# Additions of whole graphs by accumulating DMAs, and one more halving of row sums, in a four-layer graph network on one core

## The chip, the cores and the metric

The kernel runs on one core of a Trainium2 chip. Times are device microseconds (us). A core has five engines that run side by side, each working through its own instructions in a fixed order: TensorE (PE, matrix products; PEld is its weight load), VectorE (DVE), ScalarE (ACT), GpSimd (POOL) and SyncE (SP, which only issues DMAs here). An engine waits for others by semaphores. DMAs are issued by SP and POOL and are carried out by 16 DMA engines. [...]

## The reference

32 graphs of 512 nodes with 256 features pass through four layers. They share one adjacency matrix of 512 by 512. Each layer's output is added to its input and normalised over the features.

```python
# layer 0: attention with 8 heads, then a two-layer perceptron, each with residual and layernorm
scores = jnp.where(mask, jnp.einsum('fnhd,fmhd->fhnm', q, k) / jnp.sqrt(D), -1e9)
t = jnp.einsum('fhnm,fmhd->fnhd', jax.nn.softmax(scores, axis=-1), v).reshape(F, N, C)
x = _layernorm(x + t, ln1_g, ln1_b)
h = jax.nn.relu(jnp.einsum('fnc,cd->fnd', x, w1) + b1)
x = _layernorm(x + jnp.einsum('fnd,dc->fnc', h, w2) + b2, ln2_g, ln2_b)
...
# layer 1: e = leaky_relu(s1[n] + s2[m]), masked softmax, times h, one head
# layer 2: e = leaky_relu(h1 h2^T), masked softmax, times h3, relu
# layer 3: as layer 1 with 4 heads of 64 features, then elu
...
# around every layer
x = _layernorm(x + layer(x))
```

## The kernel before

One graph is held as tiles of 128 partitions: a tile [128, 4, 256] has node 128c + p of the graph in partition p and part c. One such tile (kinds "x" and "y") is 512 KB. Attention weights of four blocks are held as a tile [128, 4, 512] of kind "p", 1 MB. Everything is float32, and every product is made of two records of PE. A PSUM bank ("bank") takes one result of [128, 512].

`graph(b)` loads one graph by SP, runs `layer0` to `layer3`, each followed by `normalise`, and stores the result by SP. `normalise` takes statistics on DVE (L906, L907), a power of -1/2 on POOL (L909, L910), a product on DVE (L911), and applies them on ACT (L914).

What belongs to the change:

- `add` (L918) is an addition or product on POOL of two of the four parts of a tile, so a whole tile takes two. It is used in layer 0 for the residual (`t + xs`), for `xs + be2_row`, for `n1 * g1_row` and for `y + bb_row`; in layers 2 and 3 for the residual (`y + xs`). The result is read by DVE: by the statistics L906, by L1085 (`f = product + y`), by L1095 (`f + xs`), and by L1279 (the last step of the elu in layer 3).
- `add_dma` (L927) adds one "p" tile to another by an accumulating DMA of 1 MB issued by POOL. Layer 0 uses it to sum the exponentials over the blocks of source nodes (six times a graph), layer 3 twice a graph.
- The row sums of the softmax are column sums of those totals over the partitions, made on PE: L1041 in layer 0 and L1266 in layer 3. In layer 3 a total holds two blocks of two heads each, and eight products with 32 columns of weights (`pick`) leave the two blocks of a head in separate rows. After a transposition `rinv3` adds the two on DVE (L960) and takes the reciprocal (L964).
- The product of weights and values is L1024 in layer 0 (32 columns of weights each) and L1251 in layer 3 (64 columns each). The attention scores of layer 0 are L995 (32 rows). All other products use the whole array.

The order of work is not that of the program text. Every step is handed to `plan` with its engine, a price in ns, what it reads and writes, for some a `lag` (how long after the issue the result is believed to be there) and for PE a number `tiling` for the mode of the array. `Plan.place` then simulates the engines and writes down their order: it takes the engine that can start first, and on it the step with the earliest start and, among equals, the earliest due time. A step whose `tiling` differs from the mode that PE is in has `STAY` added to its due time, and is believed to cost 100 ns more. Up to `WAYS` = 5 graphs are in flight; graph b + 5 begins when graph b has ended. Due times come from `PACE`, `TENTHS` and `LAST`, first starts from `START`. On the chip the engines keep this order and wait for the true ends of what they need.

Before the graphs, `prepare` loads weights and the adjacency (`load`, L727) and derives tables from them, among them edge_t from transpositions at L766 and a product of two weights of layer 2 from transpositions at L830.

Of the kernel before, what the change touches and what calls it, by code (L numbers as in the profile page):

```python
# [13 lines left out]
ALU = mybir.AluOpType  # L14
# [3 lines left out]
P = 128  # L18
# [8 lines left out]
WAYS = 5  # L27
PACE = 94.27
START = (0, 0, 51.94, 76.72, 152.79)
LAST = ()  # L30
STAY = 4.37
TENTHS = (0, 52.5, 93.97, 124.51, 191.84, 234.11, 292.66, 343.39, 414.47, 446.08, 504.73)
@with_exitstack
# [578 lines left out]
def fast_path(  # L612
# [86 lines left out]
    def T(slot):  # L699
        return slot.tile if slot.kind is None else buffers[slot.kind][slot.index]  # L700
# [25 lines left out]
    def prepare():  # L726
        def load(dst, to, src, lag=3000):  # L727
            def run():
                with nc.allow_non_contiguous_dma(reason="columns, once"):
                    nc.sync.dma_start(to(T(dst[0] if isinstance(dst, tuple) else dst)), src)  # L730
            plan(SP, 60, run, [], [dst], lag=lag)

# [193 lines left out]

    def add_dma(dst, src):  # L927

        plan(POOL, 950, lambda: nc.gpsimd.dma_start(T(dst), T(src), accum_op=ALU.add),  # L929
             [src, dst], [dst], lag=7000)  # L930

# [21 lines left out]
    def rinv3(sm):  # L953


        bank, rinv = sums_back(sm), Slot("ri")

        def run():
            r = T(rinv)[:, :NC * H3]
            nc.vector.tensor_reduce(  # L960
                r.rearrange("p (c k i) -> p c k i", c=NC, k=KC),
                T(bank).rearrange("p (c a i r) -> p c r i a", c=NC, a=2, i=2)[:, :, 0:KC],
                mybir.AxisListType.X, ALU.add)
            nc.vector.reciprocal(r, r)  # L964
        dve(400, run, [bank], [rinv])
        return rinv
# [36 lines left out]
    def layer0(xs):  # L1003
# [47 lines left out]
        dve(370, check, [rinv], [], True)  # L1051
        for c0 in range(0, NC, 2):
            add(t, t, xs, c0)
        n1 = Slot("y")
        normalise(t, n1)
        for c0 in range(0, NC, 2):
            add(xs, xs, None, c0, be2_row)
        nT = transposed(n1)
        y = Slot("y")
        for c0 in range(0, NC, 2):  # L1060
            add(y, n1, None, c0, g1_row, ALU.mult)
            add(y, y, None, c0, bb_row)
        hT = Slot("t")
# [36 lines left out]
    def gates(v, heads, G):  # L1100
# [5 lines left out]
        def check():  # L1106
# [11 lines left out]
            [bank], [gT])  # L1118
        plan(SP, 60, lambda: nc.sync.dma_start(T(row)[:R, :], T(gT)[:R, :]), [gT], [row], lag=2000)
        if heads == 1:  # L1120
            to = lambda: T(G)
        else:
            to = lambda: flat(T(G))
        plan(SP, 60, lambda: nc.sync.dma_start(
            to(), T(row)[:R, :].rearrange("r q -> (r q)").partition_broadcast(P)),
            [row], [G], lag=2300 + 1100 * heads)
        e1, e02 = Slot("e1"), Slot("e1")
# [35 lines left out]
    def layer2(xs):  # L1163
# [40 lines left out]
        for c0 in range(0, NC, 2):  # L1204
# [10 lines left out]
            for j in range(2):  # L1215
                act(470, lambda bank=bank, j=j, c=c0 + j: nc.scalar.activation(
                    T(y)[:, c, :], T(bank)[:, j * C:(j + 1) * C], AF.Relu,
                    scale=T(rinvs[c])[:, 0:1]), [bank, rinvs[c0 + j]], [(y, c0 + j)])
            add(y, y, xs, c0)
        return y  # L1220

    def layer3(xs):
# [5 lines left out]
        for k in range(KC):  # L1228
            av = Slot("bank")
            for m0 in range(0, NC, 2):  # L1230
# [16 lines left out]
                def run(p=p, m0=m0, k=k, av=av):  # L1247
                    for m in range(2):
                        for i in range(2):
# [4 lines left out]
                                             stop=(m0 + m == NC - 1))  # L1254
                plan(PE, 1770, run, [q, p], [av], tiling=2)
                if m0 == 0:
                    total = p
                else:
                    add_dma(total, p)

            totals.append(total)
            evac(oT, lambda t, k=k: t[:, k, :], av, lambda b: b, N, [(oT, k)])
        def run():
            for k, p in enumerate(totals):
                for j in range(4):
                    nc.tensor.matmul(T(sm)[32 * j:32 * j + 32, :], pick[:, k, :], T(p)[:, j, :],  # L1266
                                     start=(k == 0), stop=(k == KC - 1))
        plan(PE, 1740, run, totals, [sm], tiling=2)
        t = heads_out(oT, rinv3(sm), H3)

        e, y = Slot("y"), Slot("y")
        for c0 in range(0, NC, 2):
            w, parts = slice(c0, c0 + 2), (c0, c0 + 1)
            act(600, lambda w=w: nc.scalar.activation(T(e)[:, w, :], T(t)[:, w, :], AF.Exp),
                [(t, c) for c in parts], [(e, c) for c in parts])
            act(600, lambda w=w: nc.scalar.activation(T(y)[:, w, :], T(t)[:, w, :], AF.Relu),
                [(t, c) for c in parts], [(y, c) for c in parts])
            add(y, y, xs, c0)
            dve(790, lambda w=w: nc.vector.scalar_tensor_tensor(  # L1279
                T(y)[:, w, :], T(e)[:, w, :], 1.0, T(y)[:, w, :], ALU.min, ALU.add),  # L1280
                [(s, c) for s in (y, e) for c in parts], [(y, c) for c in parts], True)
        return y

    def graph(b):
        xs = Slot("x")
        plan(SP, 60, lambda xs=xs: nc.sync.dma_start(
            T(xs), x[b].rearrange("(c p) d -> p c d", p=P)), [], [(xs, c) for c in range(NC)],
            lag=11000)
        for layer in (layer0, layer1, layer2, layer3):
            y = layer(xs)  # L1290
            xs = Slot("x")
            normalise(y, xs)
        plan(SP, 60, lambda: nc.sync.dma_start(
            out[b].rearrange("(c p) d -> p c d", p=P), T(xs)), [xs], [], lag=3000)
# [79 lines left out]
```

## Time and profile before

| | |
|---|---|
| median of 3 runs | 3067.17 us (3066.87 to 3067.29) |
| profiled execution | 3065.91 us |
| its span, first to last instruction | 3064.1 us |
| mean granted TensorE clock | 0.989 |
| PE idle in the span | 120 us |
| DVE busy | 2313.2 us (75%) |
| POOL busy | 1368.9 us (45%) |

The page has one line per engine with its busy time, its share of the span and its number of instructions, then the span in 40 slices with the busy share of each in tenths, then groups of instructions: source line, engine, operation, output and input, shapes and count, busy us, mean ns of one, and after the second bar the idle time just before them with what ended most of it. DMA issues show the size of one and the median time from issue to landing.

Three facts help in reading it. A group's line can be that of a helper: all of POOL's additions have L921. A POOL record of a DMA is the time of its issue, not of the transfer. And idle time of an engine that sets no end costs nothing.

### The profile page before, as it was taken

How to read it: one execution, taken by the hardware profiler on the slowest of the kernel's cores; microseconds unless marked ns; L12 is line 12 of the kernel's file. 1: busy time of each engine (PE TensorE's matmuls, PEld its weight loads, DVE VectorE, ACT ScalarE, POOL GpSimd, SP SyncE). 2: the span in 40 equal slices, each digit the busy share in tenths (PEclk: the TensorE clock that was granted, in tenths of full speed). 3: DMA queues.
4: the chain of work that ended last, by engine and by line, in shares of the span. 5: the costliest groups of instructions: out<-in, count | busy, mean ns of one | idle time of the engine just before them, and what ended most of it. 6: DMA issues, size and time to landing. Idle time of an engine off the chain costs nothing.

```text
span 3064.1 us, 41217 instructions
## 1 busy us (share of the span) xinstructions
PE 2943.6 (96%) x14954; PEld 1650.4 (54%) x14954; DVE 2313.2 (75%) x4170; ACT 1890.3 (62%) x3975; POOL 1368.9 (45%) x1195
## 2 busy tenths in 40 slices
PE   6989999999999999999999999999999999999994
PEld 3455555555555555555555555555555555555551
DVE  4667777777777777777777777778777778777774
ACT  4656666666666666666666666566766666666552
POOL 0433455444455444455444455444455444454422
PEclk9999999999999999999999999999999999999997
DMA  5644654555654555654555654555655555655323
GB/s 149 131 85 100 141 117 94 126 116 114 141 118 93 126 116 114 141 117 96 127 113 114 141 116 95 116 122 118 135 110 107 114 122 119 132 113 107 80 75 82
DMA packets 85939, 351.65 MB, mean 115 GB/s; under 512 B 7905, under 2 KB 43873, under 8 KB 48865
## 3 DMA queue, kind: packets, MB, share of 16 engines
q0 software_dynamic: 36864, 268.45, 44.6%
q1 hardware_dynamic: 48864, 80.49, 7.5%
q8 instruction: 120, 1.97, 0.3%
q14 instruction: 91, 0.74, 0.1%
HBM read 63.38 MB, written 17.10 MB: 26 GB/s over the span
## 4 chain that ended last, share of the span: by engine, by line
PE 73%; DMA 17%; DVE 5%; ACT 3%; issue 2%; POOL 0%; SPq 0%; POOLq 0%; DVEq 0%; ACTq 0%
DMA p<-p 15%; PE bank L878 9%; PE bank L892 8%; PE bank L995 8%; PE bank L1152 8%; PE bank L1211 7%; PE bank L1024 6%; PE bank L1251 6%; PE bank L1069 4%; PE bank L865 4%; PE bank L1081 4%; DVE p L1017 2%; PE bank L1266 2%; ACT p L999 2%; PE bank L978 2%; PE bank L1200 2%
## 5 line engine op out<-in xcount | busy, mean ns | idle before, releaser
L1017 DVE TENSOR_TENSOR p<-p,edge_t 128x2048 f32<-128x2048 f32 x256 | 625.5, 2446 | 225.1 <-ACT p L999 221.4
L929 POOL DMA_DIRECT2D p<-p x256 | 239.2, 935 | 895.5 <-PE bank L1251 159.8
L853 ACT ACTIVATE t<-bank 128x512 f32<-128x512 f32 x640 | 371.0, 595 | 415.7 <-PE bank L878 162.3
L999 ACT ACTIVATE p<-bank 128x512 f32<-128x512 f32 x1024 | 533.0, 603 | 99.0 <-PE bank L995 98.7
L921 POOL TENSOR_TENSOR y<-y,x 128x512 f32<-128x512 f32 x192 | 321.9, 1735 | 313.6 <-DVE y L981 239.1
L906 DVE BATCH_NORM_STATS2 st<-y 128x6 f32<-128x256 f32 x768 | 314.7, 410 | 11.4 <-POOL y L921 3.6
L995 PE MATMUL bank<-t,t 32*128 32x512 f32 x2048 | 301.8, 644 | 0.0
L1242 DVE TENSOR_TENSOR p<-p,edge_t 128x2048 f32<-128x2048 f32 x128 | 294.1, 2298 | 4.2
L914 ACT ACTIVATE x<-y,rs,rs 128x256 f32<-128x256 f32 x512 | 276.0, 591 | 25.2 <-DVE rs L911 24.2
L1235 DVE TENSOR_SCALAR p<-p,e,e 128x512 f32<-128x512 f32 x512 | 256.9, 541 | 39.6 <-DMA p<-row 39.6
L1024 PE MATMUL bank<-p,v 128*32 128x512 f32 x2048 | 269.7, 608 | 10.5 <-DVE p L1017 10.3
L1251 PE MATMUL bank<-p,v 128*64 128x512 f32 x1024 | 252.6, 615 | 22.7 <-DVE p L1242 22.6
L909 POOL TENSOR_SCALAR rs<-mv 128x4 f32<-128x4 f32 x192 | 161.5, 841 | 223.9 <-DVE mv L907 211.5
L1152 PE MATMUL bank<-v,p 128*128 128x257 f32 x1024 | 249.4, 389 | 6.9 <-DVE p L1145 6.9
L1152 PEld LDWEIGHTS bank<-v,p 128*128 128x128 f32 x1024 | 189.1, 191 | 88.7 <-issue 24.4
L1211 PE MATMUL bank<-v,p 128*128 128x256 f32 x1024 | 235.2, 383 | 0.0
L878 PE MATMUL bank<-t,wqkv 128*128 128x512 f32 x512 | 227.1, 594 | 0.0
L1177 PE MATMUL bank<-t,t 128*128 128x512 f32 x512 | 225.1, 592 | 0.0
L1211 PEld LDWEIGHTS bank<-v,p 128*128 128x128 f32 x1024 | 192.6, 191 | 47.8 <-ACT t L853 20.5
L853 ACT ACTIVATE v<-bank 128x512 f32<-128x512 f32 (+2 forms) x384 | 176.5, 461 | 64.5 <-PE bank L892 32.0
L910 POOL TENSOR_TENSOR rs<-rs,mhalf 128x4 f32<-128x4 f32 x192 | 207.6, 1081 | 16.0
L921 POOL TENSOR_TENSOR y<-y,bb_row 128x512 f32<-128x512 f32 x64 | 186.4, 2912 | 4.9
(117 smaller groups left out, 4636.7 us busy)
## 6 DMA issues: line engine op xcount, KB each, us to landing
p<-p POOLq DMA_DIRECT2D x256, 1024.0 KB, 8.0
p<-row SPq DMA_DIRECT2D x32, 1024.0 KB, 9.4
x<-in_x_dram SPq DMA_DIRECT2D x32, 512.0 KB, 8.3
out_dram<-x SPq DMA_DIRECT2D x32, 512.0 KB, 2.9
e<-row SPq DMA_DIRECT2D x32, 256.0 KB, 3.5
t<-in_adj_dram SPq DMA_DIRECT2D x4, 256.0 KB, 6.0
wqkv<-in_L_gnn_w_qkv_dram SPq DMA_DIRECT2D x1, 768.0 KB
y<-in_L_gnn_W_dram SPq DMA_DIRECT2D x2, 256.0 KB
```

Source lines behind the costliest of these rows:

```text
L853: act(170 + n * 0.84, lambda: nc.scalar.activation(to(T(dst)), frm(T(src)), AF.Copy), [src], writes)
L878: nc.tensor.matmul(T(bank), T(w)[:, i, col:col + P], T(xT)[:, i, :], start=(i == 0), stop=(i == KC - 1))
L906: nc.vector.bn_stats(T(st)[:, c, :], T(y)[:, c, :])
L921: pool(1500 if row is None else 1850, lambda: nc.gpsimd.tensor_tensor(T(dst)[:, w, :], T(a)[:, w, :], T(b)[:, w, :] if row is None else T( ...
L995: nc.tensor.matmul(T(banks[j]), T(kT)[r, g, m * P:(m + 1) * P], T(qT)[r, g, :], start=True, stop=True)
L999: act(600, lambda j=j: nc.scalar.activation(T(p)[:, j, :], T(banks[j]), AF.Exp, scale=1.0 / math.sqrt(D0)), [banks[j]], [(p, j)])
L1017: dve(2420, lambda p=p, m=m: nc.vector.tensor_tensor(T(p), T(p), T(edge_t)[:, m, :].unsqueeze(1).to_broadcast([P, J, N]), ALU.mult), [p, ( ...
L1024: nc.tensor.matmul(T(av)[j * D0:(j + 1) * D0, :], T(v)[:, m, h * D0:(h + 1) * D0], T(p)[:, j, :], start=(m == 0), stop=(m == NC - 1))
L1152: nc.tensor.matmul(T(bank)[:, :C + 1], T(p)[:, m, c * P:(c + 1) * P], T(v)[:, m, 2:C + 3], start=(m == 0), stop=(m == NC - 1))
L1211: nc.tensor.matmul(T(bank)[:, j * C:(j + 1) * C], T(pT)[:, m, c * P:(c + 1) * P], T(v)[:, m, :C], start=(m == 0), stop=(m == NC - 1))
L1242: nc.vector.tensor_tensor(p4, p4, T(edge_t)[:, m0:m0 + 2, :].unsqueeze(2).to_broadcast([P, 2, 2, N]), ALU.mult)
L1251: nc.tensor.matmul(T(av)[i * D3:(i + 1) * D3, :], T(q)[:, m0 + m, 2 * H3 + h * D3:2 * H3 + (h + 1) * D3], T(p)[:, 2 * m + i, :], start=(m0 ...
```

## The change

- `add_dma` can now take a whole tile of kind "x" or "y", a row that is repeated for all four parts (`row=True`), or no source: then it adds blocks 2 and 3 of a tile to its blocks 0 and 1.
- Five additions of each graph that POOL made in two halves each become one accumulating DMA of 512 KB: `t + xs`, `xs + be2_row` and `y + bb_row` in layer 0, `y + xs` in layers 2 and 3. The product with `g1_row` stays on POOL.
- In layer 3 each of the two totals is halved once more by an accumulating DMA of 512 KB, issued behind the first. The row sums then take four products instead of eight, and `rinv3` takes the reciprocal alone.
- L1251 has a mode number of its own for the planner (`tiling=3`).
- The planner's prices change: an SP issue from 60 to 450 ns; the default lag of weight loads from 3 to 15 us; a graph's load from 11 to 9 us; accumulating DMAs from 7 to 7.5 us (1 MB) and 5.5 (512 KB); the broadcast of a row of gates from 2300 + 1100 per head to 1500 + 1900 per head. `PACE`, `START`, `LAST`, `STAY` and `TENTHS` have new values.

```diff
-PACE = 94.27
-START = (0, 0, 51.94, 76.72, 152.79)
-LAST = ()
-STAY = 4.37
+PACE = 97.38
+START = (0, 0, 23.42, 89.7, 132.67)
+LAST = (0.95, 0, 4.11, 0)
+STAY = 7.12
...
-        def load(dst, to, src, lag=3000):
+        def load(dst, to, src, lag=15000):
...
-            plan(SP, 60, run, [], [dst], lag=lag)
+            plan(SP, 450, run, [], [dst], lag=lag)
...
-    def add_dma(dst, src):
-
-        plan(POOL, 950, lambda: nc.gpsimd.dma_start(T(dst), T(src), accum_op=ALU.add),
-             [src, dst], [dst], lag=7000)
+    def add_dma(dst, src, row=False, lag=7500):
+
+        def run():
+            a = T(dst) if src else T(dst)[:, 0:2, :]
+            b = T(src) if src else T(dst)[:, 2:4, :]
+            nc.gpsimd.dma_start(a, b.unsqueeze(1).to_broadcast([P, NC, C]) if row else b,
+                                accum_op=ALU.add)
+        plan(POOL, 950, run, [src, dst] if src else [dst], [dst], lag=lag)
...
-        def run():
-            r = T(rinv)[:, :NC * H3]
-            nc.vector.tensor_reduce(
-                r.rearrange("p (c k i) -> p c k i", c=NC, k=KC),
-                T(bank).rearrange("p (c a i r) -> p c r i a", c=NC, a=2, i=2)[:, :, 0:KC],
-                mybir.AxisListType.X, ALU.add)
-            nc.vector.reciprocal(r, r)
-        dve(400, run, [bank], [rinv])
+        dve(250, lambda: nc.vector.reciprocal(
+            T(rinv)[:, :NC * H3], T(bank).rearrange("p (s r) -> p s r", r=32)[:, :, 0]),
+            [bank], [rinv])
...
-        for c0 in range(0, NC, 2):
-            add(t, t, xs, c0)
+        add_dma(t, xs, lag=5500)
...
-        for c0 in range(0, NC, 2):
-            add(xs, xs, None, c0, be2_row)
+        add_dma(xs, be2_row, True, 5500)
...
             add(y, n1, None, c0, g1_row, ALU.mult)
-            add(y, y, None, c0, bb_row)
+        add_dma(y, bb_row, True, 5500)
...
-            add(y, y, xs, c0)
+        add_dma(y, xs, lag=5500)
...
-                plan(PE, 1770, run, [q, p], [av], tiling=2)
+                plan(PE, 1770, run, [q, p], [av], tiling=3)
                 if m0 == 0:
                     total = p
                 else:
                     add_dma(total, p)
+                    add_dma(total, None, lag=5500)
...
-            for k, p in enumerate(totals):
-                for j in range(4):
-                    nc.tensor.matmul(T(sm)[32 * j:32 * j + 32, :], pick[:, k, :], T(p)[:, j, :],
-                                     start=(k == 0), stop=(k == KC - 1))
-        plan(PE, 1740, run, totals, [sm], tiling=2)
+            for h in range(H3):
+                nc.tensor.matmul(T(sm)[32 * h:32 * h + 32, :], pick[:, 0, :],
+                                 T(totals[h // 2])[:, h % 2, :], start=True, stop=True)
+        plan(PE, 870, run, totals, [sm], tiling=2)
...
-            add(y, y, xs, c0)
-            dve(790, lambda w=w: nc.vector.scalar_tensor_tensor(
+        add_dma(y, xs, lag=5500)
+        for c0 in range(0, NC, 2):
+            w, parts = slice(c0, c0 + 2), (c0, c0 + 1)
+            dve(690, lambda w=w: nc.vector.scalar_tensor_tensor(
                 T(y)[:, w, :], T(e)[:, w, :], 1.0, T(y)[:, w, :], ALU.min, ALU.add),
                 [(s, c) for s in (y, e) for c in parts], [(y, c) for c in parts], True)
```

## The prediction

> **What bounds the kernel now.** I read the page's first two parts (busy times, and the span in 40 slices), then the table of stages, then the groups of instructions, the waits and the end of the chain.
>
> ```profile
> span 3064.1 us, 41217 instructions
> PE 2943.6 (96%) x14954; PEld 1650.4 (54%) x14954; DVE 2313.2 (75%) x4170; ACT 1890.3 (62%) x3975; POOL 1368.9 (45%) x1195
> ...
> PE   6989999999999999999999999999999999999994
> ```
>
> ```profile
> 0.00:20.00 20.00, 1.40 (x7) 1.43 (x8) 2.82 (x9) 1.94 (x3) 1.09 (x11) 1.00 0.88 262
> 500.00:700.00 200.00, 198.50 (x1035) 111.61 (x1035) 155.54 (x279) 129.51 (x271) 97.59 (x82) 1.00 0.54 116
> 3020.00:3040.00 20.00, 12.96 (x42) 2.94 (x42) 15.11 (x18) 1.19 (x2) 1.84 (x2) 0.70 0.50 112
> ```
>
> The columns of a stage are its length, then busy us of PE, PEld, DVE, ACT and POOL, the granted clock, the DMA share and GB/s. TensorE (PE) is the bound: it idles 120 us of 3064 (3064.1 - 2943.6). Adding the stages, about 39 us of that lie before 200 us, 46 after 2900, and only 35 in the 2600 us between, where a graph leaves every 92.2 us (outputs start at 447.80 and 2844.87, 26 graphs apart). So in the middle only three things move the time: PE work, PE's own overhead, and new waits of PE. GpSimd (POOL), at 45%, is no bound.
>
> ```profile
> L921 POOL TENSOR_TENSOR y<-y,x 128x512 f32<-128x512 f32 x192 | 321.9, 1735 | 313.6 <-DVE y L981 239.1
> L921 POOL TENSOR_TENSOR y<-y,bb_row 128x512 f32<-128x512 f32 x64 | 186.4, 2912 | 4.9
> L929 POOL DMA_DIRECT2D p<-p x256 | 239.2, 935 | 895.5 <-PE bank L1251 159.8
> ...
> p<-p POOLq DMA_DIRECT2D x256, 1024.0 KB, 8.0
> ```
>
> ```profile
> PE bank L1041 <- DMA p<-p: 22.0, 24, 3.5
> ```
>
> ```profile
> q0 software_dynamic: 36864, 268.45, 44.6%
> ```
>
> These are groups and DMA issues of the page, one line of the waits (us, times, longest) and one of the queues. To be seen: what POOL's additions cost, what an accumulating DMA costs POOL (0.935 us) and until it lands (8.0 us), and that the one steady wait of PE that is of any size, 22.0 of 35 us, is already a wait for accumulating DMAs, at the row sums of layer 0.
>
> **What the Trainium skill says.** "TensorEngine Tiling (Array Packing)", Key Properties: changing the tiling mode drains TensorE. The trace agrees: eight records of L1024 take 0.99 us to the next start when another mode follows (1500.92 to 1501.91), sixteen in one mode take 1.86 (1528.71 to 1530.57), so eight without a change cost 0.87 and a change about 0.12 us. "DMA: Bandwidth & Descriptors", Anatomy of one DMA, gives 2.0 us plus bytes over 436e3 for a DMA from GpSimd: 4.4 us for 1 MB. The trace has 8.0, so I use the trace's. The same section says that DMA engines do not wait on semaphores, the issuing sequencer does; the trace agrees: POOL stood 157.7 us in 35 waits of an accumulating DMA for the one before. "GPSIMD Engine Reference", Specifications, says GpSimd's SBUF interface is shared with VectorE; L1279, which runs beside POOL's additions, took from 657 to 1755 ns, which fits.
>
> **The change part by part.**
>
> *Row sums of layer 3 (L1266).* 16 records a graph become 8. At 1514.27 sixteen take 1.83 us to the next start; eight, with the same change of mode behind them, cost the 0.99 of above. Saved 0.84 us on the bound engine, times 32: **-27 us**. No cover can hide a saving on PE in the middle. The DVE reduction L960 (0.19 us each) goes too, on an engine at 75%: nothing.
>
> *The second halving and five whole-graph additions.* Per graph POOL loses ten additions, in the groups 321.9 + 186.4 + 128.8 = 637 us in all, and issues seven more DMAs, 224 x 0.935 = 209 us: POOL falls to about 941 us (31%). The two DMAs that repeat a row have 1 KB pieces instead of 4 KB; their issue is not in the trace. Bounds: 0.85 us (the shortest issue seen) to 3.7 (four times 0.935, if it goes by pieces); I take 0.935. At the upper end POOL gets 64 x 2.8 = 180 us back, still under 37%. Nothing on PE either way.
>
> *Their landing.* q0's share makes 0.446 x 3064.1 / 256 = 5.34 us of all 16 engines for 1 MB, so an 8.0 us landing (shortest 6.9) is 5.34 plus 1.6 to 2.7. For 0.5 MB: 2.67 plus the same, 4.3 to 5.3; the page's fit would give 3.2 as a lower end, the 1 MB row 8.0 as the upper. I take 5.3. The load of q0 goes from 8 x 5.34 = 42.7 us a graph to 42.7 + 7 x 2.67 = 61.4, 64% of the time, or 67% if small pieces cost half as much again; with SP's queue the engines go from 0.54 to about 0.74.
>
> *The chain of one graph.* A residual that POOL added pair by pair behind its producer (1.7 us, the next instruction already beginning on the first pair) now waits for all four parts and 5.3 us. Three of these lie on the graph's chain (after layer 0's attention, after layers 2 and 3), about +4.5 us each; the bias rows lie beside transposes and two products (L1069 and L1081, over 7 us of PE) and are covered. The halving adds 5.3. So a graph's chain grows by some 19 us. Five graphs are in flight, and one stays 452 us (363.26 to 815.43), while graph 0 went through in 356 us with less company (1.75 to 357.38): in the middle there is slack, so nothing is charged there. At the end there is none:
>
> ```profile
> 3035.69 7.06 DMA p<-p
> 3042.80 1.98 PE bank L1266 x8
> ...
> 3049.41 1.27 POOL y L921
> 3050.71 2.34 DVE y L1279 x2
> ```
>
> The halving puts 5.3 us behind 3042.75 and takes 1.0 from L1266: +4.3. The last residual goes from 3049.41 + 1.27 to a DMA issued at about 3050.4 and landed at 3055.7, then two L1279 at 0.69: 3057.1 where it was 3053.05, +4. Layer 2's residual of the last graph, on the chain at 2994.35, adds 4.5; the L1266 at 3001.62 gives 1.7 back, and some rearranging I put at 1: **+10 us**.
>
> *The order.* It is written by the planner from its prices, so every changed price reorders all engines. Two effects can be priced. First, weights: loads at default lag are now believed to land at 15 us plus 0.45 per issue, not 3 plus 0.06. PE's first instruction now waits for such a load until 18.60 (L830), while x of graph 0 (issued 1.75, 8.3 us to landing) and the adjacency (last L758 at 9.49, 0.43 long) were there at about 10. With the new prices those come first: up to -8.5 us of starting delay, if the ramp hands it on. Bounds 0 and -8.5; I take **-7**. Second, L1251 (64 columns) now counts as its own mode. In the listing of PE from 1499.53 to 1592.1 I count 30 changes of mode, 3 of them between L1251 and the 32-column ones, which the old planner took for none. Half of them saved: 1.5 x 0.12 x 32 = 6; it could also cost as much. I take **-3**. The prices of SP's issues add no instruction: nothing on the chip.
>
> *New waits in the middle.* DVE now waits for DMAs at L906, L1085, L1095 and L1279 where it waited for POOL; queued behind a waiting DVE are L1017 and L1242, which PE needs. PE waits at L1266 for a longer row of DMAs. On POOL, the powers L910 stand behind any issue that waits for a DMA. The new lags (7.5 us for 1 MB, 5.5 for 0.5, each behind 0.95 of issue: 8.45 and 6.45) lie above 8.0 and 5.3, so the order leaves room for some lateness. Bounds: -10 (the present 22.0 us at L1041 half gone) to +70 (below). I take **+2**.
>
> Sum: -27 + 10 - 7 - 3 + 2 = **-25 us**. The profiled execution took 3065.91 (its span 3064.1 and 1.8 around it): 3041. The median shown is 1.3 above that one: 3042.
>
> **The rivals.** *The DMAs become PE's wait* (the slower side). q0 serves one accumulating DMA behind another; in this profile a sum at 1545.42 took 11.32 us and the one chained to it 8.23. At 64% instead of 45% such lateness is more usual, and PE keeps its order. Price: L1041's wait doubles (0.7 us a graph, 22.0 / 32), L1266 gets one of 1.0, and three late residuals on DVE pass 0.3 on: 2.0 x 32 = 64 us. With -27 - 7 - 3 + 10 this makes +37: 3104. It decides from 0.84 us a graph (27 us), where it eats the sums. For it: 1545.42. Against it: L1266 waited for a DMA only at the very end, 3.0 us.
>
> *The gain is only handed back*: added waits of about 0.8 us a graph, or a ramp that keeps none of the 7 us and an end longer by 15. Within 6 us of 3067.
>
> *The new order is much better*: of 30 changes of mode a graph five go (0.6 us x 32 = 19), and the last graphs spread their load: 3042 - 24 = 3018. For it: a change costs 0.12 us, 30 of them 3.6 of 92.2. Against: most follow from the work itself.
>
> That the change doesn't do what it says is out for the sums: L1266's loop is over four heads instead of eight tiles.
>
> **How the numbers follow.** Forecast (3042, own range 3026 to 3058) 0.48; better order (3018) 0.13; handed back 0.11; DMAs as the wait (3104, spread 3075 to 3120) 0.28. This measurement can tell about 0.2%, 6 us. Faster: 0.61; same 0.11; slower 0.28. For 8 in 10 I cut half of the better order's lower tail and about half of the slow case: 3012 to 3100.
>
> **What would show it.** Right: L1266 at x256 with about half of 63.5 us; PE busy near 2943.6 - 30; PE's first record near 10 us; q0 near 64%; POOL near 31%; a graph every 91.2 us or less in the middle; the tail from the last sums to the end longer by 8. Wrong: PE's idle time between 300 and 2900 well over 35 us with p<-p or y as releaser, or DVE idle for DMA at L906 and L1279 and PE behind it at L1024 or L1251.

## The result, and the profile after

| | before | after |
|---|---|---|
| median | 3067.02 us (3066.82 to 3067.29, 4 runs) | 3244.72 us (3243.13 to 3244.84, 4 runs) |
| profiled execution / span | 3065.91 / 3064.1 us | 3244.68 / 3242.9 us |
| mean granted clock | 0.989 | 0.962 |
| PE busy, idle in the span | 2943.6, 120.5 us | 2986.1, 256.8 us |

The ratio is 1.0578 [1.056, 1.0596]: the kernel became 5.8% slower, where 0.8% faster was forecast. The lines moved a little: L1266 (row sums of layer 3) is now L1261, L1251 is L1246, L1017 is L1014, L929 (the accumulating DMAs) is L932, L1279 is L1276; L906 to L921 stayed.

First the page of after: its span and busy times, q0's line, one group, and four of the DMA issues (number, size, median us from issue to landing).

```profile
span 3242.9 us, 41072 instructions
PE 2986.1 (92%) x14698; PEld 1670.9 (52%) x14698; DVE 2232.2 (69%) x4138; ACT 1865.5 (58%) x3975; POOL 960.8 (30%) x1099
...
q0 software_dynamic: 93696, 385.91, 62.0%
...
L1261 PE MATMUL bank<-p,pick 128*32 128x512 f32 x256 | 85.5, 769 | 142.8 <-DMA p<-p 142.8
...
y<-x POOLq DMA_DIRECT2D x96, 512.0 KB, 5.4
...
p<-p POOLq DMA_DIRECT2D x64, 512.0 KB, 8.9
...
x<-be_row POOLq DMA_DIRECT2D x32, 512.0 KB, 5.2
y<-bb_row POOLq DMA_DIRECT2D x32, 512.0 KB, 11.4
```

The work is what the prediction counted: 256 records fewer on PE, POOL at 30%, q0 at 62%, L1261 with 256 records. Yet PE is busy 42.5 us longer with fewer records, and idle 136 us longer. The row sums of layer 3 have half the records and are busy 85.5 us, where the prediction expected half of 63.5; a record takes 769 ns on the mean instead of 613 (before). A transfer of 512 KB lands in 5.2 to 5.4 us in one place of the program and in 8.9 or 11.4 in another.

A stage of the middle (its length, busy us of PE, PEld, DVE, ACT and POOL, clock, DMA share, GB/s) and the waits of after (us, times, longest):

```profile
500.00:700.00 200.00, 184.27 (x918) 103.19 (x916) 141.06 (x259) 115.83 (x248) 61.05 (x68) 0.98 0.74 149
```

```profile
PE bank L1261 <- DMA p<-p: 142.8, 31, 9.0
...
DVE st L906 <- DMA y<-x: 108.9, 30, 6.4
```

In the same 200 us, PE was busy 198.5 before and is busy 184.3 now, with 918 records instead of 1035. Most of the loss lies in the middle, in every graph: between 300 and 2800 us PE idles 155 us (2500 - 2344.7; before 30). Both big waits come about once a graph, 31 and 30 times, and both are for accumulating DMAs, those that add to what stands at their destination.

One such place in the timeline (start, us, engine, line, operation; in brackets the idle time before it and its releaser). First POOL of after, where every DMA record is an issue:

```profile
1570.69 0.85 POOL L932 DMA_DIRECT2D p<-p  x1 [3.90 <-DMA p<-p]
...
1574.52 0.94 POOL L932 DMA_DIRECT2D p<-p  x1 [1.57 <-issue]
1575.12 1.24 POOL L932 DMA_DIRECT2D y<-x  x1
1575.67 1.58 POOL L932 DMA_DIRECT2D p<-p  x1
```

By the program's order these are: the halving of the graph's first total; a 1 MB sum of layer 0 of another graph; the residual of layer 2 of a third; and the halving of the second total. Then PE, and the stages around its stop:

```profile
1582.88 1.03 PE L1261 MATMUL bank<-p,pick 128*32 128x512 f32 x4
1588.17 1.92 PE L1261 MATMUL bank<-p,pick 128*32 128x512 f32 x4 [4.27 <-DMA p<-p]
1590.03 2.09 PE L992 MATMUL bank<-t,t 32*128 32x512 f32 x8
...
1599.08 1.14 PE L992 MATMUL bank<-t,t 32*128 32x512 f32 x8
```

```profile
1582.00:1588.00 6.00, 1.91 (x12) 0.38 (x12) 2.91 (x9) 0.00 (x0) 0.00 (x0) 0.94 1.06 193
1588.00:1591.00 3.00, 2.83 (x8) 0.74 (x12) 1.34 (x1) 0.60 (x1) 0.89 (x1) 0.50 0.81 127
1591.00:1594.00 3.00, 3.00 (x14) 1.44 (x7) 0.69 (x4) 0.00 (x0) 0.00 (x0) 0.50 1.06 216
1594.00:1598.00 4.00, 4.00 (x22) 1.88 (x21) 2.23 (x7) 2.55 (x6) 1.27 (x2) 0.99 0.52 104
```

The second halving was issued at 1575.67 and PE goes on at 1588.17, 12.5 us later, and 13.65 after the first issue of the three (1574.52). Three transfers put at q0 within 1.2 us need 5.34 + 2.67 + 2.67 = 10.7 us of all 16 engines, and the landing of a single one lies 1.6 to 2.7 above its transfer: 12.3 to 13.4, if the queue was empty. It was not quite, since the first halving landed only 7.1 us after 1570.69. The residual (issued 1575.12) held DVE up as well: its next L906 starts at 1585.45 after 2.95 us of waiting, and PE goes on 2.72 us after that, the time of one transfer of 512 KB. All this fits a queue that serves its transfers one after the other, in the order of issue. PE stood 4.27 us, and then paid again: for some 6 us the granted clock is 0.50, and the eight records of L992 take 2.09 us where at 1599.08 they take 1.14, the four of L1261 1.92 where they take 1.03 at 1582.88.

The place is typical. In the graphs between 400 and 2800 us the second halving lands 11.4 to 13.9 us after its issue, where one that finds the queue empty takes 4.5 to 4.6 (e7 and e9 below). The delay of 6.8 us or more is longer than PE's stop there, 4.0 to 5.9, so queueing alone can account for the whole stop. The median of 8.9 on the page mixes these with the first halvings, which land after 7.1 to 9.5.

The end became longer, too: the last row sums of L1261 wait 9.02 us and start at 3215.67, 27.2 us before the end; before, L1266 left 21.3 (3042.80 to 3064.1).

### The profile page after: what moved, and what is told of

Read it like the earlier page. It is cut to its first block, busy times and chain, and to the rows that moved or that the text cites. A ratio compares the mean times of both kernels' runs of the same rounds, so it can differ in the third digit from the quotient of the medians.

```text
span 3242.9 us, 41072 instructions
## 1 busy us (share of the span) xinstructions
PE 2986.1 (92%) x14698; PEld 1670.9 (52%) x14698; DVE 2232.2 (69%) x4138; ACT 1865.5 (58%) x3975; POOL 960.8 (30%) x1099
## 5 line engine op out<-in xcount | busy, mean ns | idle before, releaser
L1014 DVE TENSOR_TENSOR p<-p,edge_t 128x2048 f32<-128x2048 f32 x256 | 608.8, 2380 | 131.6 <-ACT p L996 131.5
L932 POOL DMA_DIRECT2D p<-p x320 | 305.2, 957 | 1103.6 <-PE bank L1246 275.2
L853 ACT ACTIVATE t<-bank 128x512 f32<-128x512 f32 x640 | 380.0, 602 | 301.9 <-PE bank L878 160.9
L906 DVE BATCH_NORM_STATS2 st<-y 128x6 f32<-128x256 f32 x768 | 312.5, 407 | 111.7 <-DMA y<-x 108.9
L992 PE MATMUL bank<-t,t 32*128 32x512 f32 x2048 | 319.2, 692 | 0.0
L1021 PE MATMUL bank<-p,v 128*32 128x512 f32 x2048 | 271.1, 609 | 28.2 <-DVE p L1014 28.2
L1237 DVE TENSOR_TENSOR p<-p,edge_t 128x2048 f32<-128x2048 f32 x128 | 292.9, 2289 | 3.4
L1230 DVE TENSOR_SCALAR p<-p,e,e 128x512 f32<-128x512 f32 x512 | 247.7, 541 | 15.8 <-DMA p<-row 15.8
L1246 PE MATMUL bank<-p,v 128*64 128x512 f32 x1024 | 239.0, 608 | 18.9 <-DVE p L1237 18.9
L910 POOL TENSOR_TENSOR rs<-rs,mhalf 128x4 f32<-128x4 f32 x192 | 249.0, 1297 | 13.8
L1261 PE MATMUL bank<-p,pick 128*32 128x512 f32 x256 | 85.5, 769 | 142.8 <-DMA p<-p 142.8
L909 POOL TENSOR_SCALAR rs<-mv 128x4 f32<-128x4 f32 x192 | 122.0, 635 | 320.5 <-DVE mv L907 224.6
L853 ACT ACTIVATE e<-bank 128x512 f32<-128x512 f32 x64 | 38.2, 597 | 272.6 <-PE bank L1261 252.1
## 6 DMA issues: line engine op xcount, KB each, us to landing
y<-bb_row POOLq DMA_DIRECT2D x32, 512.0 KB, 11.4
```

The costliest lines, as they stand in the source:

```text
L853: act(170 + n * 0.84, lambda: nc.scalar.activation(to(T(dst)), frm(T(src)), AF.Copy), [src], writes)
L906: nc.vector.bn_stats(T(st)[:, c, :], T(y)[:, c, :])
L910: pool(1040, lambda: nc.gpsimd.tensor_tensor(T(rs), T(rs), mhalf, ALU.pow), [rs], [rs])
L932: nc.gpsimd.dma_start(a, b.unsqueeze(1).to_broadcast([P, NC, C]) if row else b, accum_op=ALU.add)
L992: nc.tensor.matmul(T(banks[j]), T(kT)[r, g, m * P:(m + 1) * P], T(qT)[r, g, :], start=True, stop=True)
L1014: dve(2420, lambda p=p, m=m: nc.vector.tensor_tensor(T(p), T(p), T(edge_t)[:, m, :].unsqueeze(1).to_broadcast([P, J, N]), ALU.mult), [p, ( ...
```

## The experiments

The theories, by the letters that the expectations use:

- Q: q0 serves its accumulating DMAs in turn, so the halving lands late behind a sum and a residual of other graphs, and PE waits for it.
- S: an extra hop between the sum and the row sums is too long, whatever else is queued.
- G: GpSimd's additions, if they come back, take up what is gained.
- D: the residual DMAs hold PE up by way of VectorE (L906).
- P: the fault is the lag in the planner; with a longer one the order has room.
- O: with a longer lag, or a landing moved, the next instruction in the chain is late instead.

Runs e1 to e8 rest on one execution each, beside executions of before of 3065 to 3073; e9 to e12 on four or five each. Except where it says otherwise, each keeps the order of instructions that the planner wrote for after.

### e2 and e12: the halving not issued

```diff
+            if not src:
+                return
...
-                nc.tensor.matmul(T(sm)[32 * h:32 * h + 32, :], pick[:, 0, :],
-                                 T(totals[h // 2])[:, h % 2, :], start=True, stop=True)
+                for m in range(2):
+                    nc.tensor.matmul(T(sm)[32 * h:32 * h + 32, :], pick[:, 0, :],
+                                     T(totals[h // 2])[:, 2 * m + h % 2, :], start=(m == 0), stop=(m == 1))
```

> The order of the changed kernel is kept, but the second halving is not issued and the row sums of layer 3 take eight products again; the five additions stay DMAs. Theory Q and rival S alike: the wait at L1261 goes to under 20 us, PE idle in the middle falls by 4 us a graph and the clock comes back to 0.98 or more; PE work rises by 27 us; span 3060 to 3110. Rival D (the residuals by DMA, which VectorE waits for, hold PE up as well): span above 3150, with PE waiting behind L906, L1014 or L1237.

> e2 again, timed: its one time of 3051 stood beside 3071 of the kernel before. If the residuals by DMA and the new order gain by themselves, the ratio is 0.990 to 0.997; an interval that holds 1 would say that the one look was luck.

e2 took 3051.04; the same kernel over four executions, e12, took 3052.23 (3051.78 to 3054.17), ratio to before 0.9943 [0.9927, 0.996]. So everything else in the change together, the residuals by DMA and the new order, makes the kernel 0.6% faster, and the halving with its four products turns that into 5.8% slower. The wait for a DMA is gone from the row sums of layer 3, but for 3.8 us once, though q0 is still at 59.9%: so high a share need not make PE wait.

### e11: four products, no halving

As e12, but with the four products of after. Half of each total, and so half of the source nodes, is left out of the row sums.

```diff
-                for m in range(2):
-                    nc.tensor.matmul(T(sm)[32 * h:32 * h + 32, :], pick[:, 0, :],
-                                     T(totals[h // 2])[:, 2 * m + h % 2, :], start=(m == 0), stop=(m == 1))
+                nc.tensor.matmul(T(sm)[32 * h:32 * h + 32, :], pick[:, 0, :],
+                                 T(totals[h // 2])[:, h % 2, :], start=True, stop=True)
```

> As e2 (order of the changed kernel, second halving not issued), but with four products instead of eight: the row sums of layer 3 then leave out one block in two of the source nodes. It measures the term of the prediction by itself, PE's work saved at the row sums: 27 us below e2 if PE is the bound throughout (ratio to before about 0.986), less if PE then stands longer at its next wait.

It took 3053.37 (3053.19 to 3057.42), ratio 0.9947 [0.9931, 0.9964]: no different from e12. PE's busy time did fall, from 2927.6 to 2907.2, but its idle time rose by more than that in the profiled executions (148.3 after 124.7). Where it went shows in the waits of e12, then of e11:

```profile
PE bank L977 <- DVE ri L962: 10.6, 12, 1.8
```

```profile
PE bank L977 <- DVE ri L962: 32.9, 24, 2.5
```

L977 multiplies by the reciprocal that DVE makes from these sums. PE comes to it earlier, but DVE gets to L962 hardly earlier in its own order. The saving on the bound engine was real work removed, and in this order it was worth nothing, where 27 us were expected.

After differs from e11 by the halving DMA alone, and both have 14698 records on PE. The difference of 191 us (3244.72 - 3053.37) is therefore that DMA's, and in the profiled executions it divides into 108.5 us more idle time (256.8 - 148.3) and 78.9 us more busy time for the same records (2986.1 - 2907.2), with the mean clock at 0.962 instead of 0.983. In the traces the clock is at 0.50 for 251 us of after and 103 of e11, and PE is busy in 179 and 63 us of these. A record at half clock takes about twice as long, so by this estimate the clock accounts for some 58 of the 79 us ((179 - 63) / 2); the rest stays open.

### e5: the halving issued, but nothing waits for it

As e12, but with the halving DMA at its place in the program, adding into a spare tile that nobody reads. There is one such tile for all halvings.

```diff
+            if not src:
+                nc.gpsimd.dma_start(spare, T(dst)[:, 2:4, :], accum_op=ALU.add)
+                return
```

> As e2 (order of the changed kernel, eight products of row sums), but each second halving is issued at its place and adds into a spare tile that nothing reads, so the queue carries the same load and GpSimd waits and issues as in the changed kernel, and only PE's wait for the halving is gone. If the dependence (PE standing at L1261 and the clock that falls after it) is the cost: within 30 us of e2's 3051. If the load of the queue and of GpSimd is the cost: 3120 or more.

3132.62: 80 us over e12 with nothing waiting for its result. q0 is at 64.2%. The spare DMA itself lands 8.7 us after its issue, and what stands behind it lands later in turn: DVE's wait for residuals (L908 here, L906 in e12) goes from 68.1 to 104.1 us, and behind DVE the same reciprocal as above is late. The waits of e5:

```profile
PE bank L980 <- DVE ri L965: 45.2, 16, 3.5
```

So of the 192 us between e12 and after, up to 80 come from the load on the queue, by way of VectorE, and the other 112 or more (3244.72 - 3132.62) go with PE's own wait for the halving. The 80 are not the load alone: as the spare tile is shared, GpSimd stands 79.3 us, in 24 waits, for one halving before it issues the next, which it needn't in after. How the 192 us divide is therefore known only roughly.

### e6: the halving issued ahead of its neighbours

The halving is issued ahead of other accumulating DMAs that the plan had placed up to 2.5 us before it. No work is removed.

```diff
+            for j in range(i - 1, -1, -1):
+                if seq[j][0] < t - near:
+                    break
+                if seq[j][1] is op.source:
+                    break
+                if seq[j][1].role == "other":
+                    to = j
+            if to < i:
+                seq.insert(to, seq.pop(i))
```

> As the changed kernel, with one thing moved: where GpSimd issued other accumulating DMAs within 2.5 us ahead of a second halving, the halving is issued ahead of them (at 1575.67 a 1 MB sum of layer 0 and a residual stood before it). Theory Q: the halving lands in 4.5 to 6.5 us instead of 8.9, the wait at L1261 falls from 142.8 to under 40 us, and the time is e2's 3051 less the 27 us of PE work: 3025 to 3060. Rival S (the hop is too long for its place in any case): the wait stays above 80 us and the time above 3140.

The landing came as theory Q has it: in the middle the second halving lands after 4.7 to 6.4 us instead of 11.4 to 13.9 (median of all 6.3 instead of 8.9), and the halving is nearly gone from PE's waits (14.6 us, 10.2 of it in the last graphs). The time did not: 3236.97, where Q had 3025 to 3060. In the timeline of e6, at the place shown for after, the halving now goes out in the first record, which holds two DMAs, and the residual comes last:

```profile
1571.54 1.85 POOL L953 DMA_DIRECT2D p<-p  x2 [3.65 <-issue]
1572.69 1.58 POOL L953 DMA_DIRECT2D y<-x  x1
...
1584.24 0.43 DVE L927 BATCH_NORM_STATS2 st<-y 128x6 f32<-128x256 f32 x1 [4.75 <-DMA y<-x]
...
1588.05 0.25 DVE L983 RECIPROCAL ri<-bank 128x16 f32<-128x16 f32 x1
1588.36 0.65 PE L998 MATMUL bank<-ident,t 128*128 128x128 f32 x4 [2.42 <-DVE ri L983]
```

The residual issued at 1572.69 is there 11.5 us later. DVE stands 4.75 us for it, everything queued behind it is late, the reciprocal too, and PE waits for that (103.7 us in 24 waits in the whole run). Swapping the order of issue swapped who is late: this is the clearest sign that the queue serves in order. The time of three transfers doesn't go away by being given to another of the three.

### e1 and e8: the five additions back on GpSimd

e1 keeps the halving, e8 leaves it out as e12 does.

```diff
+            if row or (src and src.kind in ("x", "y")):
+                for w in (slice(0, 2), slice(2, 4)):
+                    nc.gpsimd.tensor_tensor(
+                        T(dst)[:, w, :], T(dst)[:, w, :],
+                        T(src).unsqueeze(1).to_broadcast([P, 2, C]) if row else T(src)[:, w, :], ALU.add)
+                return
```

> The order of the changed kernel is kept, but the five additions of whole graphs are made by GpSimd in place, in two halves each; the second halving stays a DMA. Theory Q (one queue serves the accumulating DMAs in turn, and the residual ahead of the second halving is part of what delays it): q0 falls from 62% to about 50%, the halving lands in 6 to 8 us instead of 8.9, the wait at L1261 falls from 142.8 us to 40 to 90, span 3130 to 3190. Rival S (the extra hop alone is too long for the place that the order gave to the sums, whatever else is in the queue): the wait at L1261 stays within 20 us of 142.8. Rival G (the additions on GpSimd take up the gain, since each holds GpSimd's queue for 3 us where an issue held it for 1): span above 3230.

> The order of the changed kernel with both parts undone in place: the second halving is not issued and the row sums take eight products, and the five additions of whole graphs are made by GpSimd in two halves each. Beside e2 (3051) this gives what the residual DMAs are worth where no halving crowds the queue. If they pay by themselves, through GpSimd's and VectorE's time: 3070 to 3120, with L1014 slower than in e2, as in e1 (2761 ns against 2380). If their traffic only costs: 3020 to 3045.

| in the order of after | residuals by DMA | residuals on GpSimd |
|---|---|---|
| halving | 3245 | 3171 (e1) |
| no halving | 3052 (e12) | 3151 (e8) |

In e1 PE's wait for a DMA at the row sums fell to 12.6 us in 4 waits, less than the 40 to 90 expected, and q0 to 47.7%. The second halving of a graph lands after 8.6 to 9.8 us between 400 and 2700 us, some 3 to 4 sooner than in after: about the one transfer of 2.67 us that stood before it, as Q has it. But that it is no longer PE's wait has a second reason. Just before the row sums PE now stands for VectorE. GpSimd's sum and second halving, then PE, and one of PE's waits, all of e1:

```profile
1542.62 0.93 POOL L938 DMA_DIRECT2D p<-p  x1
...
1545.70 1.23 POOL L938 DMA_DIRECT2D p<-p  x1
...
1554.09 1.94 PE L1027 MATMUL bank<-p,v 128*32 128x512 f32 x8 [4.23 <-DVE p L1020]
1555.80 1.94 PE L1267 MATMUL bank<-p,pick 128*32 128x512 f32 x8
```

```profile
PE bank L1027 <- DVE p L1020: 121.3, 36, 4.3
```

While PE stands for 4.23 us the halving lands. So the 20 us that it costs here (3171 against 3151) are not its price where nothing else holds PE up, and this run doesn't decide against S. What speaks against S in the middle of after is that a landing without a queue takes 4.5 us, as reckoned above.

GpSimd's additions cost 98 us (3151 against 3052; at most 3120 was expected). Why can be seen in a group of e8 and the same one of e12:

```profile
L1022 DVE TENSOR_TENSOR p<-p,edge_t 128x2048 f32<-128x2048 f32 x256 | 681.5, 2663 | 62.7 <-ACT p L1004 62.7
```

```profile
L1016 DVE TENSOR_TENSOR p<-p,edge_t 128x2048 f32<-128x2048 f32 x256 | 601.2, 2350 | 125.6 <-ACT p L998 125.0
```

The same VectorE instruction takes 2663 ns in the one and 2350 in the other. In e8, 137 of the 256 have no TENSOR_TENSOR of GpSimd beside them, the kind that its additions are, and take 2257 to 2294 ns; the other 119 take 3108 on the mean and up to 6250. PE waits for it (97.3 us at L1029 in e8; 21.7 in e12). DVE is busy 2416.8 us against 2216.0. This order was written for DMAs, so 98 us is not what they gain over the kernel before, where the additions had their own places; e12 against before says that, 0.6% with the new order included.

### e3: a longer lag for the halving

Here the planner writes a new order, with the settings unchanged.

```diff
-                    add_dma(total, None, lag=5500)
+                    add_dma(total, None, lag=12000)
```

> Only the planner's lag of the second halving changes, from 5.5 to 12 us, near what it took in the middle (12.5 us from issue to the sums at 1575.67). Theory P (the price is the fault, not the work): the order puts L1261 later, its wait falls under 40 us, span 3050 to 3100, below 3067 if nothing else waits. Rival O (with q0 at 62% whatever comes next in the order is late too): the wait moves to L1038, L906 or L1014 and the span stays above 3150.

3194.85. The wait at the row sums is gone (11.7 us in 2 waits), but PE now waits at L1021 for DVE, and DVE for residuals and for rows of gates. The waits of e3:

```profile
PE bank L1021 <- DVE p L1014: 113.7, 80, 3.8
...
DVE y L1276 <- DMA y<-x: 80.5, 27, 6.9
```

A residual lands after 9.1 us at the median, where the plan has 5.5. One longer lag repairs one place and leaves the others wrong: theory O. The settings weren't fitted to the new lag either, so with a new search the same lag might do better.

### e7: the halving alone, in the order of before

Before's order and prices, residuals on GpSimd; only the halving is added, placed 8 us behind its sum, with four products.

```diff
+                while late and (late[0][0] <= t or op is late[0][1]):
+                    late.pop(0)[2]()
                 op.run()
+                if op.half:
+                    late.append((t + 8000, op.sums, op.half))
...
-        plan(PE, 1740, run, totals, [sm], tiling=2)
+            for h in range(H3):
+                nc.tensor.matmul(T(sm)[32 * h:32 * h + 32, :], pick[:, 0, :],
+                                 T(totals[h // 2])[:, h % 2, :], start=True, stop=True)
+        last = plan(PE, 1740, run, totals, [sm], tiling=2)
```

> The kernel before in its own order with its own prices, residuals on GpSimd, and only the second halving added: it is issued 8 us after the sum that it needs was placed (or right before the row sums if these come sooner), and the row sums take four products. The sum landed some 2 us before L1266 in the kernel before, so the halving lands 3 to 4 us after it. If a hop that the order has no room for costs whatever is in the queue: PE waits at the row sums 2 to 4 us a graph, and 3110 to 3220. If the residuals' traffic is what makes the halving dear: 3040 to 3080.

3150.80 beside 3067.16. PE waits 64.7 us in 33 waits for the halving. Its median landing of 4.7 us suggests a hop for which the order left no room, theory S. But the median mixes two sorts. The first halving of a graph finds the queue empty and lands after 4.5 us or little more. The second, for which PE waits, is issued behind a 1 MB sum, as here in e7:

```profile
1541.28 0.88 POOL L936 DMA_DIRECT2D p<-p  x1
...
1545.33 0.87 POOL L1260 DMA_DIRECT2D p<-p  x1 [1.87 <-DMA p<-p]
...
1553.44 1.05 PE L1268 MATMUL bank<-p,pick 128*32 128x512 f32 x4 [1.46 <-DMA p<-p]
```

Between 400 and 2900 us it lands after 6.7 to 8.8 us, 2.2 to 4.3 more than alone, and PE waits 0.7 to 2.7 us for it. In all but one of these graphs the delay in the queue is longer than the wait. So Q has a share here too, at 49%; that of S is clear only at the end, where the halving lands in 4.6 us and PE yet waits 19 us in five waits.

### e4: the old work in the new prices and settings

The work of before, with the lags, issue prices and `PACE`, `START`, `LAST`, `STAY` and `TENTHS` of after, and a new order from these.

> The kernel before with the changed kernel's prices and settings (SP issues, lags of loads and rows, 7.5 us for 1 MB, the mode number of L1251, PACE, START, LAST, STAY, TENTHS), and none of the new DMAs. If the new work is the cause: span 3040 to 3080, with PE starting at about 10 us. If the new settings are the cause: span above 3150.

3419.04, slower than either kernel, with PE idle 333 us in waits of every kind. The expectation took that for a sign that the settings are at fault. But settings that were searched for one set of operations needn't fit another, so this run can't say whether the new work or the new prices are at fault. e12 can, since it keeps the order of after and is fast.

### e9 and e10: one queue in the plan

If the cause is a plan that takes each DMA for independent, a plan with a queue must mend most of it. The planner now keeps the time at which q0 is free: a transfer begins when it is issued and the one before is through. `PACE`, `START` and the others were searched anew for it. e9 has all of the change; e10 leaves out the halving, with eight products as in e12.

```diff
+            if op.xfer:
+                queue = max(queue, t + op.ns) + op.xfer
+                done = queue + op.lag + SIGNAL
...
-    def add_dma(dst, src, row=False, lag=7500):
+    def add_dma(dst, src, row=False, xfer=5340):
...
-        plan(POOL, 950, run, [src, dst] if src else [dst], [dst], lag=lag)
+        plan(POOL, 950, run, [src, dst] if src else [dst], [dst], lag=1200).xfer = xfer
...
-        add_dma(t, xs, lag=5500)
+        add_dma(t, xs, xfer=2670)
...
-        add_dma(xs, be2_row, True, 5500)
+        add_dma(xs, be2_row, True, 2900)
```

> All of the change is kept, but the planner now knows that GpSimd's DMAs share one queue: each takes 5.34 us of it for 1 MB, 2.67 for 512 KB (2.9 with a repeated row), in order of issue, and lands 1.27 us after its turn; the settings are searched anew under this price. Theory Q: with room made for the bunches the halving pays its 27 us: PE's wait for DMAs is under 40 us, VectorE's at L906 under 60, and 3000 to 3050. If the load of the queue cannot be placed at all beside five graphs in flight: above 3067.

> As e9, also with settings searched anew, without the second halving (eight products of row sums). PE has 27 us more to do and the queue 17% less. Theory Q expects it behind e9, by 10 to 30 us (3020 to 3070); if the halving is dear even with room made for it, this one is the faster.

e9: 3079.48 (3077.32 to 3085.2), ratio 1.0042 [1.0027, 1.0056]. The same DMAs and the same four products as after, 165 us less, and q0 at 64.5%. The halving lands in 4.8 us. But by its own expectation (3000 to 3050) the run missed: it lies above 3067, where the rival had it, and the halving doesn't pay its 27 us. PE's largest wait is now at the row sums of layer 0, which wait for accumulating DMAs as well. The waits of e9:

```profile
PE bank L1042 <- DMA p<-p: 59.5, 28, 4.4
```

e10: 3011.52 (3009.8 to 3013.59), ratio 0.9816 [0.98, 0.9833], faster than before and after. Q had expected it 10 to 30 us behind e9; it is 68 ahead (3079.48 - 3011.52), so the halving is dear even with the queue in the plan, as far as two separate searches of settings can show it. Its middle, in the columns of the stages above:

```profile
300.00:2800.00 2500.00, 2495.89 (x12857) 1426.96 (x12856) 1888.53 (x3523) 1607.01 (x3441) 737.41 (x888) 1.00 0.71 149
```

PE idles 4 us of 2500 and keeps its full clock. How much of the 165 us between after and e9, and of the 41 between e12 and e10, is the queue's price in the plan and how much the new search of settings isn't told apart: a search with the fixed lags wasn't run beside them.

## Why the prediction was wrong

The step that failed is the term for new waits in the middle: "lie above 8.0 and 5.3, so the order leaves room for some lateness ... I take **+2**". It set a median landing against the plan's lag, as if each DMA met an empty queue. But the same text had said that q0 serves one DMA behind another. (Its example, the 11.32 us of a sum at 1545.42, was misread: nothing else was in q0 then, and SP's queue was moving a row of 1 MB, issued at 1546.27, and an output, issued at 1550.75, on the same engines. The sum at 1597.69, 3.3 us behind another and landed after 10.95, would have shown the queue.) With fifteen DMAs a graph instead of eight, three within 2.5 us come in 20 graphs of 32, in before in none, and the second halving lands after 11.4 to 13.9 us in the middle against a plan of 6.45. This happens in every graph, as the order repeats. The runs put the halving DMA at +191 (after against e11), up to 80 by its load on the queue (e5), the rest with PE's wait for it. The upper bound of +70 on this term was too low by a factor of nearly three.

The rival "the DMAs become PE's wait" named the mechanism and the place: L1266, and L906 on DVE. Its price, 2.0 us a graph, was wrong. The wait at L1261 alone is 4.6 us each time (142.8 / 31). And no case priced what a stop does to the clock: the 79 us by which the same PE records take longer in after than in e11, some 58 of them by the estimate above. It would have had to be 6 us a graph (191 / 32), not two.

Point by point:

- Row sums, -27: three quarters of the work went (20 us of PE busy time, e12 to e11), the time didn't (+1 us, within what these runs can tell). "No cover can hide a saving on PE in the middle" was wrong: PE, in its fixed order, waits a few instructions later for the reciprocal. The first question should have been who must act between the shortened step and PE's next step.
- Chain of one graph, nothing charged in the middle because five graphs are in flight: wrong for the halving. PE keeps its order, so a graph's slack doesn't help where a landing is later than the order allows: PE waits for it once a graph in after, and in e7 without the residual DMAs. For the residuals alone it held (e12).
- Start, -7: right in direction and too small. PE's first record is at 7.49 us instead of 18.60, and by 200 us it has 180.2 us of work behind it instead of 161.0. What of these 19 us reached the end wasn't measured alone; e12 as a whole gains some 18 us on the executions of before beside it (3052.23 against 3069.81).
- End, +10: about right. From the last row sums to the end it is 5.9 us longer (27.2 against 21.3), and the last row sums themselves wait 9.02 us instead of 3.00.
- Changes of mode, -3: not earned. Between 500 and 1500 us PE's records change mode 334 times before and 334 times after; with 98.6 us a graph instead of 92.2 that is 33 a graph instead of 31. The direct changes between 32 and 64 columns went from 31 to none, and others came for them.
- Landing of 512 KB, 5.3: right as a median (5.2 and 5.4 in two groups); with nothing ahead it is 4.5, and 5.2 for a repeated row, whose issue takes 1.3 us instead of the 0.935 taken.
- GpSimd relieved, "nothing on PE either way": wrong, on the other side. Relief of POOL reaches PE through DVE, whose instructions get shorter: 98 us in the order of after (e8 against e12), which was written for DMAs. It didn't save the forecast, since the queue took more.
- q0, POOL and the count of L1261 came out as foretold.

The signs to look for served: idle time of PE between 300 and 2900 well over 35 us with p<-p as releaser was the mark of the rival, and it is what the profile shows.

## What to carry to other kernels

Price a shared DMA queue as one more engine, with a service time for each transfer and an order, and look for bunches, before moving work to it: with two or three transfers ahead, the landing of a single one says little, and a median over places of different kinds hides the late ones. A stop of the bound engine in every round costs more than its length where the clock drops behind it, and a saving on the bound engine is worth nothing if the next thing that it waits for doesn't come sooner. After a change of work or prices, an order that was searched should be searched again before the change is judged: with the queue in the plan and settings searched anew the whole change came to +0.4% instead of +5.8%, and without its halving to -1.8%.

## What the runs showed of the hardware

- After PE had stood for 4.27 us up to 1588.17, the granted clock was 0.50 for about 6 us, then 0.99; in the whole kernel equal records took 79 us longer than in e11. All 25 stops of 4.0 to 5.9 us between 400 and 2800 us in after had 3.4 or 6.8 us at half clock at or just after their end. The Trainium skill describes this, in "TensorE: Matmul & The Clock Gate", section "HAM oscillation — how this bites in real kernels": a wait for a DMA beyond some 3.4 us makes PE go on at half clock, and the cost is paid in every round. The trace agrees, and the prediction, which used another page on TensorE, didn't charge it. The runs show it after shorter stops, too: in e7 six of twelve stops of 2.0 to 2.8 us were followed by 3.4 us or more at half clock.
- q0 served its accumulating DMAs in order of issue: 12.5 us for the last of 1 MB, 512 KB and 512 KB, and the lateness changed hands when the order of issue was changed (e6). The Trainium skill, "DMA: Bandwidth & Descriptors", section "Two DMAs through the same engine are not ordered", says that descriptors of one queue of one engine start in order, though an earlier one need not have finished writing when a later one completes; the order of starts fits.
- GpSimd's additions beside them lengthened VectorE's instructions, as the split of e8's 256 multiplications shows. On the mean, from e12 to e8, the multiplication by the edges of layer 0 went from 2350 to 2663 ns, the steps of layer 3 that make p from e (L1232 in e12) from 540 to 743, the multiplication of layer 3 (L1239) hardly, from 2288 to 2296.
- A repeated row in 1 KB pieces cost POOL 1.3 us to issue, in after, where the medians of the other accumulating DMAs are 0.9 to 1.2; it landed at best after 5.2 us where a whole tile took 4.5.
